# A graph layer's bias moved from TensorE to GpSimd, one slice product by seven, and a reordered last slice

## The chip, the cores and the metric

The kernel runs on one core of a Trainium2 chip. The metric is device time in microseconds (us), here the median of three runs. The engines are PE (TensorE, matrix products), DVE (VectorE), ACT (ScalarE), POOL (GpSimd) and SP (SyncE, which here only issues transfers). [...] All tensors are fp32, and every matmul appears in the records twice.

## The reference, cut to what matters

x is (8, 2048, 64): 8 batches, 2048 nodes, 64 features. Each of four layers computes `x = layernorm(x + layer(x, adj))`. The change concerns the first:

```python
# layer 0: A is adj (2048 x 2048), D = 16, K = 3
w = einsum('nd,dkio->nkio', embedding, weight)   # a weight of its own for each node
b = einsum('nd,do->no', embedding, bias)         # and a bias of its own
As = [eye, A, 2 * (A @ A) - eye]
x_g = einsum('knm,bmc->bnkc', stack(As), x)
out = einsum('bnki,nkio->bno', x_g, w) + b
x = layernorm(x + out)
```

Layers 1 to 3 multiply by adj five times more and project with small weights. The change does not touch them.

## The kernel before

Nodes lie on the 128 partitions in 16 tiles, and `xy[:, slot, tile, :]` holds two versions of x, with 8 batches of 64 features side by side as four pairs of 128 columns. A product with adj is computed by Strassen's method with seven products instead of eight (names A11, A12, A22, S1 to S4), and inside each of those once more by `inner`, so that 49 block products of 512 replace 64. The sums of blocks of adj that this needs are made once, while the first product runs, and kept in HBM (`comb`).

**The slices.** The first product, A x, reads adj in four slices `ns` of columns, each in four chunks `ch`. Slice 0 (`plain_slice`) is computed partly by plain products, partly by `two_level`, which computes a quarter by seven small products. Slices 1 to 3 go through `fast_slice`: A12, A22 (by `two_level`), A11 (plain, `mul`), S1, S2, S4 and S3, in this order on PE. The generator `prepare` makes the sums of adj on DVE, and stores them through POOL's queue; `fast_slice` takes it one step further with each `next(parts)`, so the order on DVE is written out by hand. The second half of slice 0's sums is made during slice 1 (`rest`). `done` adds a product in PSUM to a partial sum and writes the result `hT`; `keep_t1` stores it, `back` transposes it on PE into slot 1 of `xy` and `last_back` does that for the last two pairs after the slices end.

**The bias.** The layer's bias is made on PE: `biases` issues 16 matmuls of 16 partitions by 64 columns from `eT` and `bias0` into the two PSUM banks of `pb`, and `join_bias` adds it to a quarter of slot 0 on DVE, four times during and after the last slice (L766 to L770). Slot 0 is the accumulator of layer 0; `centered` then takes each quarter's mean off on DVE.

**The first big product and its features.** `product(1, ...)` (L1135) runs the seven `inner` products; each of these has seven groups of four matmuls of 512 columns (L277). Two banks `mm` take turns, so a bank must be read within about one group. During it, `feature0` handles 16 combinations of four tiles and one pair, in batches of 4, 4 and 8 between the `inner` products (`RUNS`, `pump.hold`). For each tile it computes the per-node weights' terms in two halves `y` (L1109, three buffers): half 0 is added to the accumulator by DVE (L1119), half 1 is scaled by ACT into one of two buffers `s` (L1123), and POOL adds `s` up and adds it to the accumulator (L1128, L1130). POOL also squares for the layernorm (L503).

**Order.** Loops are unrolled. A planner orders each engine's instructions by its own cost estimates and by program order; each engine then runs its list in order, waiting on semaphores. `tc.keep_in_program_order` puts an instruction behind the one written before it on its engine. `pump` is a queue of generators: each `pump.step` runs one step of the job in front, `pump.run(n)` runs n jobs to their end, and `hold` stops the steps.

Of the kernel before, what the change touches and what calls it, by code (L numbers as in the profile page):

```python
# [16 lines left out]
P = 128  # L17
EPS = 1e-5
GW = 512
# [85 lines left out]
def kernel(  # L105
# [6 lines left out]
    emb: bass.AP,  # L112
    embT: bass.AP,
    w_l0: bass.AP,
# [12 lines left out]
    D = emb.shape[2]  # L127
    F = b_l0.shape[1]
    B = BF // F
# [86 lines left out]
    def product(src, feature, between=None, rate=1, own=None, pin=False, runs=None, onto_slot=None, ends=False):  # L216
# [10 lines left out]
        def add(out, a, b, op=ALU.add):  # L227
            nc.vector.tensor_tensor(out, a, b, op)  # L228
            return out
# [7 lines left out]
        def inner(q, b, finish, early=None, tail=None, next_sum=None, home=None):  # L237
# [9 lines left out]
            def new():  # L247
                if places:
                    return places.pop(0)
                return sums.tile([P, TG, 2 * F], F32, tag="t", name="t", bufs=5)  # L250

            t1 = add(new(), b12, b11, ALU.subtract)
            t2 = add(new(), b22, t1, ALU.subtract)
            t3 = add(new(), b22, b12, ALU.subtract)
            t4 = add(new(), b21, t2, ALU.subtract)
            if next_sum is not None and home is None:
# [328 lines left out]
    if True:  # L585
# [48 lines left out]
        def prepare(ns, ch, outers):  # L634
# [26 lines left out]
            def raw(I, J):  # L661
                return [ch[2 * J + b][:, 2 * I + a] for a in range(2) for b in range(2)]
# [8 lines left out]
            def rq(I, J):  # L671
                return lambda c: ch[2 * J + c][:, 2 * I : 2 * I + 2]
# [11 lines left out]
            outers[A22] = inner(A22, *raw(1, 1))  # L684
            yield
            inner(A12, *raw(0, 1))
            if ns == 0:
# [3 lines left out]
                outers[A21] = inner(None, *raw(1, 0))  # L691
            outers[S1] = s1 = outer(rq(1, 0), rq(1, 1), ALU.add)
            outers[S2] = s2 = outer(sq(s1), rq(0, 0), ALU.subtract)
# [5 lines left out]
            put(S1, s1)  # L699
            yield  # L700
            put(S2, s2)
            if ns:
                inner(A11, *raw(0, 0))
            yield
            if ns:
                outers[S3] = s3 = outer(rq(0, 0), rq(1, 0), ALU.subtract)
                yield
            put(S3, s3)
            if ns == 0:
                yield  # L710
            put(S4, s4)
            yield

        with tc.tile_pool(name="p_n", bufs=4, space=PSUM) as p_n, tc.tile_pool(
            name="p_tn", bufs=2, space=PSUM
        ) as p_tn, tc.tile_pool(name="p_b", bufs=1, space=PSUM) as p_b, tc.tile_pool(
            name="xs", bufs=1
# [5 lines left out]
            for k in range(11):  # L723
                nc.tensor.matmul(rise[:, k % TG, :], zero, zero, start=True, stop=True)

            bias0 = small.tile([P, F], F32, tag="bias0", name="bias0")
            for k in range(2):
                nc.scalar.dma_start(bias0[k * F : k * F + D], b_l0)
            pb = p_b.tile([P, NT, F], F32, tag="pb", name="pb")
            e_tile = small.tile([P, TG, 4, F], F32, tag="sq", name="eT").rearrange("p t b f -> p (t b f)")  # L730
            eT = [e_tile[g // 2 * F : g // 2 * F + D, ts(g % 2, GW)] for g in range(NG)]
            for g in range(NG):
                nc.scalar.dma_start(eT[g], embT[:, ts(g, GW)])

            def biases():

                for t in (h * NT // 2 + k for k in range(NT // 2) for h in range(2)):
                    g = t // TG
                    tc.keep_in_program_order(nc.tensor.matmul(
                        pb[:, t, :], eT[g][:, ts(t % TG, P)], bias0[g // 2 * F : g // 2 * F + D],  # L740
                        start=True, stop=True,
                    ))
                yield

            def xq(h, c):
# [12 lines left out]
            def sums_of_x(n):  # L758
# [5 lines left out]
                pin(nc.vector.tensor_tensor(out, a, b, ALU.subtract))  # L764

            def join_bias(h, c):  # L766
                v = xq(h, c).rearrange("p t h (b f) -> p (t h) b f", f=F)
                bias = pb[:, h * NT // 2 : (h + 1) * NT // 2, :].unsqueeze(2)
                bias = bias.to_broadcast([P, NT // 2, B // 2, F])
                tc.keep_in_program_order(nc.vector.tensor_tensor(v, v, bias, ALU.add))  # L770

# [35 lines left out]
            ]  # L807
            t1 = [[by_tiles(xy[:, 1, c:NT:TG, ts(n, 2 * F)]) for n in range(4)] for c in range(2)]
            b4 = [T[3][:, 2 * j : 2 * j + 2, :, ts(p, 2 * F)] for j in range(2) for p in range(2)]
# [86 lines left out]
            def fast_slice(ns, ch, held, rest):  # L896
# [16 lines left out]

                def mul(ps, a, b, start=True, steps=2):

                    for p in range(2):
                        for k in range(NT // 2):
                            nc.tensor.matmul(  # L918
                                ps[:, ts(p, GW // 2)], b(k, p), a(k // TG, k % TG),
                                start=(start and p == k == 0), stop=(k == NT // 2 - 1),  # L920
                                skip_group_check=True,
                            )
                        if p < steps:
                            pump.step()
                    return ps
# [17 lines left out]

                next(parts)
                for _ in rest:
                    pass
# [10 lines left out]
                next(parts)  # L957
                pa = mul(bank(), raw(0, 0), x_of(0, 0))
                p1 = sums.tile([P, GW], F32, tag="p1", name="p1")
                nc.scalar.copy(p1, pa)  # L960
                nc.vector.tensor_tensor(q3, q3, p1, ALU.add)
                done(0, p2, p1)
                if ns == TG - 1:
                    join_bias(0, 1)
                next(parts)
# [3 lines left out]
                if ns == 1:  # L969
                    sum_weights(w3)  # L970
                elif ns == TG - 1:
                    join_bias(0, 0)
                pb_ = mul(bank(), summed(S2), t_of(2))
                u2 = plus("u2", pb_, p1)
                nc.vector.tensor_tensor(u2, pc, u2, ALU.add)
                nc.vector.tensor_tensor(p1, pc, p1, ALU.add)
                next(parts)
                pe = mul(bank(), summed(S4), x_of(1, 1))
                done(1, pe, u2)
                if ns == TG - 1:  # L980
                    join_bias(1, 0)
                mul(pb_, summed(S3), t_of(3), start=False)

                done(2, pb_, q3)
                done(3, pb_, p1)
                return [hT[p] for p in range(NP)]

            last_pairs = []
            for ns in range(TG):
                ch = [chunks.pop((ns, j)) for j in range(NG)]  # L990
                if ns == 0:
                    outers = {}
                    parts = prepare(ns, ch, outers)
                    for _ in range(2):
                        next(parts)
                    first4 = plain_slice(ns, ch, outers)
                    next(first4)
                    sums_of_x(0)
                    sums_of_x(1)
                    next(parts)  # L1000
                    next(first4)
                    sums_of_x(2)
                    sums_of_x(3)
                    sums_t(b4, t4)
                    next(first4)
                    next(parts)
                    hT = next(first4)
                    next(parts)
                    w3 = load_weights()
                    load_chunks(1, *AHEAD)  # L1010
                    pump.add(biases())
                else:
                    hT = fast_slice(ns, ch, held, parts if ns == 1 else ())
                for p in range(NP):
                    keep_t1(ns, p, hT[p])

                held = []
                for p in range(NP):
                    if ns == TG - 2:
                        held.append((ns, p, hT[p]))  # L1020
                    elif ns == TG - 1 and p >= NP // 2:
                        last_pairs.append(hT[p])
                    else:
                        pump.add(back(ns, p, hT[p]))
            join_bias(1, 1)
            pump.drain()
# [15 lines left out]
        if True:  # L1042
# [13 lines left out]
            pump.add(last_back())  # L1056
            for h, c in ((0, 0), (0, 1), (1, 1), (1, 0)):
                pump.add(centered(h, c))
            e_sb = l0y.tile([P, NT, D], F32, tag="e_sb", name="e_sb")
            nc.gpsimd.dma_start(e_sb, emb)  # L1060

            wn = l0y.tile([P, 3, D, F], F32, tag="wn", name="wn")
# [27 lines left out]
            def feature0(g, p, hT):  # L1090
# [7 lines left out]
                for k in range(TG):  # L1098
# [3 lines left out]

                    s = l0y.tile([P, DH, 2, F], F32, tag="s", name="s", bufs=2)
                    for h in range(2):
# [25 lines left out]
                    nc.gpsimd.tensor_tensor(acc, acc, s[:, 0], ALU.add)  # L1130
                    yield


# [132 lines left out]
```

## Time and profile before

| | us |
|---|---|
| median of 3 runs (1666.35 to 1666.91) | 1666.78 |
| the profiled execution | 1666.76 |
| its span, first to last instruction | 1665.0 |
| PE busy | 1656.7 |
| DVE busy | 965.9 |
| ACT busy | 276.0 |
| POOL busy | 246.1 |

The four slices and the products that follow stand in the profiled execution like this; the columns are busy time in us of three engines, and the mean share of the DMA engines.

| stretch (us) | what | PE | DVE | POOL | DMA |
|---|---|---|---|---|---|
| 0 to 59 | slice 0 | 57.94 | 40.79 | 9.81 | 0.88 |
| 59 to 111.1 | slice 1 | 51.79 | 48.06 | 12.70 | 1.00 |
| 111.1 to 160.5 | slice 2 | 49.40 | 33.05 | 10.41 | 0.93 |
| 160.5 to 211.7 | slice 3 | 50.86 | 41.06 | 10.99 | 0.85 |
| 211.7 to 309 | A11, S1, A12, S2 | 97.29 | 69.35 | 0.00 | 0.91 |
| 309 to 391.5 | four features | 82.50 | 45.74 | 45.00 | 0.13 |
| 391.5 to 439.8 | S4, S3 | 48.30 | 27.46 | 5.89 | 0.79 |
| 439.8 to 522.4 | four features | 82.60 | 45.77 | 45.08 | 0.12 |

Durations of single instructions overlap on PE, where one is recorded from its start to its modelled end; the time from one start to the next is what a matmul costs. In a line of the timeline, brackets give the idle time before the instruction and what ended it. In a group, the number after the bar is busy time, then the mean of one in ns, then the idle time before them.

### The profile page before, as it was taken

The page shows a single profiled execution, that of the slowest core. Times are in us where ns is not written, and L with a number is a line of the kernel's source. Part 1 is how long each engine was busy: PE and PEld are TensorE (multiplying, and loading weights), DVE is VectorE, ACT ScalarE, POOL GpSimd, SP SyncE. Part 2 cuts the span into 40 slices and gives each one's busy share as a digit, 9 for nine tenths or more (in the row PEclk, how much of TensorE's full clock was granted, in tenths as well). Part 3 has the DMA queues.
Part 4 walks back from the last instruction along what each step waited for, and adds up shares of the span by engine and source line. Part 5 has one row for each costly group of instructions (what it writes and reads, how often), then busy time and mean ns, then how long its engine had stood idle before and what let it go on. Part 6 is the DMA issues. An engine that isn't in the chain of part 4 may idle for free.

```text
span 1665.0 us, 21271 instructions
## 1 busy us (share of the span) xinstructions
PE 1656.7 (100%) x8414; PEld 1060.6 (64%) x8414; DVE 965.9 (58%) x1737; ACT 276.0 (17%) x810; POOL 246.1 (15%) x332
## 2 busy tenths in 40 slices
PE   9999999999999999999999999999999999999998
PEld 5988844444444444444454455599998455579998
DVE  5986895656456456655434365873668344453657
ACT  0200110242142144430010011220001011100001
POOL 1221200254155056550000000000000000000000
PEclk9999999999999999999999999999999999999999
DMA  8998899504503600019877867657888866678884
GB/s 318 340 383 310 316 322 326 200 26 162 205 26 129 250 26 26 26 65 364 290 266 278 304 254 257 229 218 272 291 297 299 306 209 233 230 264 294 316 311 167
DMA packets 81074, 391.56 MB, mean 235 GB/s; under 512 B 8944, under 2 KB 25584, under 8 KB 41040
## 3 DMA queue, kind: packets, MB, share of 16 engines
q1 hardware_dynamic: 68288, 346.78, 58.2%
q0 software_dynamic: 11248, 42.08, 6.7%
q10 hardware_dynamic: 1440, 1.35, 0.3%
q8 instruction: 67, 1.10, 0.3%
q14 instruction: 31, 0.25, 0.0%
HBM read 339.85 MB, written 50.33 MB: 234 GB/s over the span
## 4 chain that ended last, share of the span: by engine, by line
PE 95%; DVE 3%; DMA 1%; issue 0%; SPq 0%; DVEq 0%
PE y L1109 20%; PE mmb L277 17%; PE mma L277 12%; PE mmc L277 12%; PE mmb L270 9%; PE ps_n L918 7%; PE mma L270 6%; PE mmc L270 6%; PE z L1161 3%; PE z L1190 2%; PE ps_i L832 1%; DVE si L640 1%; DMA xy<-in_x 1%; PE pt L1152 1%; DMA bias<-in_b_l 0%; DVE so L640 0%
## 5 line engine op out<-in xcount | busy, mean ns | idle before, releaser
L277 PE MATMUL mmb<-a,t 128*128 128x512 f32 x648 | 292.0, 593 | 0.0
L1119 DVE SCALAR_TENSOR_TENSOR xy<-y,e_sb,xy 128x128 f32<-128x128 f32 x512 | 179.6, 351 | 141.2 <-PE y L1109 125.3
L277 PEld LDWEIGHTS mmb<-a,t 128*128 128x128 f32 x648 | 121.5, 190 | 145.3 <-issue 143.5
L1128 POOL TENSOR_TENSOR s<-s 128x512 f32<-128x512 f32 (+2 forms) x192 | 157.4, 820 | 333.0 <-ACT s L1123 322.8
L1123 ACT ACTIVATE s<-y,e_sb 128x128 f32<-128x128 f32 x512 | 139.3, 383 | 231.5 <-PE y L1109 231.5
L228 DVE TENSOR_TENSOR u<-mmb,p 128x512 f32<-128x512 f32 x84 | 57.9, 689 | 176.5 <-PE mmb L277 121.1
L270 PE MATMUL mmb<-t,a 128*128 128x128 f32 x1344 | 156.9, 275 | 0.0
L270 PEld LDWEIGHTS mmb<-t,a 128*128 128x128 f32 x1344 | 153.5, 192 | 0.0
L1109 PE MATMUL y<-wn,xT 64*128 64x512 f32 x512 | 131.5, 590 | 0.0
L1109 PE MATMUL y<-wn,C 64*128 64x512 f32 x512 | 131.2, 589 | 0.0
L1109 PE MATMUL y<-wn,tT 64*128 64x512 f32 x512 | 131.2, 589 | 0.0
L277 PE MATMUL mma<-a,T 128*128 128x512 f32 x256 | 115.5, 594 | 0.0
L277 PE MATMUL mmc<-a,t 128*128 128x512 f32 x216 | 97.3, 592 | 0.0
L295 ACT COPY p<-mma 128x512 f32<-128x512 f32 x42 | 24.7, 588 | 405.8 <-PE mma L277 248.4
L1109 PEld LDWEIGHTS y<-wn,xT 64*128 64x128 f32 x512 | 49.3, 187 | 61.2 <-issue 60.7
L1109 PEld LDWEIGHTS y<-wn,tT 64*128 64x128 f32 x512 | 49.6, 187 | 60.2 <-issue 60.2
L1109 PEld LDWEIGHTS y<-wn,C 64*128 64x128 f32 x512 | 49.5, 187 | 60.3 <-issue 60.3
L277 PE MATMUL mma<-a,xy 128*128 128x512 f32 x192 | 86.6, 594 | 0.3 <-PE pt_n L465 0.3
L277 PEld LDWEIGHTS mma<-a,T 128*128 128x128 f32 x256 | 47.6, 190 | 56.8 <-issue 56.5
L228 DVE TENSOR_TENSOR C<-mmc,C 128x512 f32<-128x512 f32 x48 | 33.2, 692 | 85.9 <-PE mmc L277 75.1
L277 PEld LDWEIGHTS mmc<-a,t 128*128 128x128 f32 x216 | 40.0, 190 | 45.4 <-issue 45.2
L277 PEld LDWEIGHTS mma<-a,xy 128*128 128x128 f32 x192 | 36.0, 190 | 44.4 <-issue 43.8
(160 smaller groups left out, 2127.5 us busy)
## 6 DMA issues: line engine op xcount, KB each, us to landing
a<-comb SPq DMA_DIRECT2D x240, 1024.0 KB, 4.8
a<-in_blocks SPq DMA_DIRECT2D x54, 1024.0 KB, 4.8
comb<-si POOLq DMA_DIRECT2D x28, 1024.0 KB, 6.2
a<-in_slices SPq DMA_DIRECT2D x15, 1024.0 KB, 9.0
comb<-so POOLq DMA_DIRECT2D x15, 512.0 KB, 9.6
t1T<-hT SPq DMA_DIRECT2D x16, 256.0 KB, 4.6
xT<-in_xT SPq DMA_DIRECT2D x16, 256.0 KB, 3.0
tT<-t1T SPq DMA_DIRECT2D x16, 256.0 KB, 3.1
```

The lines of the kernel that those rows point to most:

```text
L228: nc.vector.tensor_tensor(out, a, b, op)
L270: nc.tensor.matmul(to, a[:, k, m, :], xb[:, m, :], start=(start and opens and m == 0), stop=(m == TG - 1), skip_group_check=True,)
L277: nc.tensor.matmul(ps, xb[:, m, :], a[:, :, m, :], start=(start and m == 0), stop=(m == TG - 1), skip_group_check=True,)
L295: nc.scalar.copy(p1, pa)
L640: tc.keep_in_program_order(nc.vector.tensor_tensor(out, a, b, op))
L918: nc.tensor.matmul(ps[:, ts(p, GW // 2)], b(k, p), a(k // TG, k % TG), start=(start and p == k == 0), stop=(k == NT // 2 - 1), skip_group_ ...
L1109: mm = nc.tensor.matmul(y[:, b, :], terms[n][half, ts(k, P)], wn[half, n, h * DH : (h + 1) * DH, :], start=(n == 0), stop=(n == 2),)
L1119: nc.vector.scalar_tensor_tensor(acc, y[:, :, ts(d, F)], e, acc, ALU.mult, ALU.add)
L1123: nc.scalar.activation(s[:, d], y[:, :, ts(d, F)], AF.Copy, scale=e)
L1128: nc.gpsimd.tensor_tensor(s[:, :n], s[:, :n], s[:, n : 2 * n], ALU.add)
L1161: nc.tensor.matmul(z[:, k, :], aT[:, ts(k, P)], wd[:, w, :], start=(n == 0), stop=(n == len(terms) - 1),)
L1190: nc.tensor.matmul(z[n][:, k], xT[half, ts(k, P)], w[half], start=True, stop=True)
```

## The change

It has four parts.

1. The bias leaves PE, `pb` and `join_bias`. `biased(h)` makes it on POOL for eight tiles: it loads the bias row to all partitions (512 KB), takes its mean off on DVE (`center`, pinned), and for each tile multiplies by the embedding, adds up the 16 terms in four steps and adds the result to the accumulator. Its two tiles are the two buffers `s` of `feature0`. `biased(0)` is a job between `centered` of the first half and of the second; `biased(1)` runs at the end of the fourth feature. The six loads of `eT` and `bias0` are gone.
2. Slice 1's A11 goes through `two_level`. Its sums and S1 are made before the rest of slice 0's sums, of which S2 and S4 are now left (S4 alone before). `t1` swaps its two places in slot 1.
3. In slice 3, S3 runs ahead of S4, in a bank of its own; pairs 0 and 1 are complete after it and are transposed during S4, which uses a `p_tn` bank. `p_tn` has four banks instead of two, in place of `pb`.
4. The four differences at the start of an `inner` with a `home` are pinned.

```diff
@@ -249,10 +248,18 @@
...
-            t1 = add(new(), b12, b11, ALU.subtract)
-            t2 = add(new(), b22, t1, ALU.subtract)
-            t3 = add(new(), b22, b12, ALU.subtract)
-            t4 = add(new(), b21, t2, ALU.subtract)
+            pin = tc.keep_in_program_order if places else lambda inst: inst
+            def less(a, b):
+                out = new()
+                pin(nc.vector.tensor_tensor(out, a, b, ALU.subtract))
+                return out
+            t1 = less(b12, b11)
+            t2 = less(b22, t1)
+            t3 = less(b22, b12)
+            t4 = less(b21, t2)
             if next_sum is not None and home is None:
@@ -683,13 +690,19 @@
...
             yield
+            if ns == 1:
+                outers[A11] = inner(A11, *raw(0, 0))
+                outers[S1] = s1 = outer(rq(1, 0), rq(1, 1), ALU.add)
+                yield
             inner(A12, *raw(0, 1))
...
                 outers[A21] = inner(None, *raw(1, 0))
-            outers[S1] = s1 = outer(rq(1, 0), rq(1, 1), ALU.add)
+            if ns != 1:
+                outers[S1] = s1 = outer(rq(1, 0), rq(1, 1), ALU.add)
             outers[S2] = s2 = outer(sq(s1), rq(0, 0), ALU.subtract)
@@ -698,22 +711,23 @@
...
             yield
+            if ns == 0:
+                put(S3, s3)
+                yield
             put(S2, s2)
-            if ns:
+            if ns > 1:
                 inner(A11, *raw(0, 0))
...
                 yield
-            put(S3, s3)
-            if ns == 0:
-                yield
+                put(S3, s3)
             put(S4, s4)
...
         with tc.tile_pool(name="p_n", bufs=4, space=PSUM) as p_n, tc.tile_pool(
-            name="p_tn", bufs=2, space=PSUM
-        ) as p_tn, tc.tile_pool(name="p_b", bufs=1, space=PSUM) as p_b, tc.tile_pool(
+            name="p_tn", bufs=4, space=PSUM
+        ) as p_tn, tc.tile_pool(
             name="xs", bufs=1
@@ -722,26 +736,6 @@
...
                 nc.tensor.matmul(rise[:, k % TG, :], zero, zero, start=True, stop=True)
-            bias0 = small.tile([P, F], F32, tag="bias0", name="bias0")
-            for k in range(2):
-                nc.scalar.dma_start(bias0[k * F : k * F + D], b_l0)
-            pb = p_b.tile([P, NT, F], F32, tag="pb", name="pb")
-            e_tile = small.tile([P, TG, 4, F], F32, tag="sq", name="eT").rearrange("p t b f -> p (t b f)")
-            eT = [e_tile[g // 2 * F : g // 2 * F + D, ts(g % 2, GW)] for g in range(NG)]
-            for g in range(NG):
-                nc.scalar.dma_start(eT[g], embT[:, ts(g, GW)])
-            def biases():
-                for t in (h * NT // 2 + k for k in range(NT // 2) for h in range(2)):
-                    g = t // TG
-                    tc.keep_in_program_order(nc.tensor.matmul(
-                        pb[:, t, :], eT[g][:, ts(t % TG, P)], bias0[g // 2 * F : g // 2 * F + D],
-                        start=True, stop=True,
-                    ))
-                yield
             def xq(h, c):
@@ -763,12 +757,6 @@
...
-            def join_bias(h, c):
-                v = xq(h, c).rearrange("p t h (b f) -> p (t h) b f", f=F)
-                bias = pb[:, h * NT // 2 : (h + 1) * NT // 2, :].unsqueeze(2)
-                bias = bias.to_broadcast([P, NT // 2, B // 2, F])
-                tc.keep_in_program_order(nc.vector.tensor_tensor(v, v, bias, ALU.add))
             def load_chunks(ns, *js):
@@ -805,7 +793,7 @@
...
             ]
-            t1 = [[by_tiles(xy[:, 1, c:NT:TG, ts(n, 2 * F)]) for n in range(4)] for c in range(2)]
+            t1 = [[by_tiles(xy[:, 1, 1 - c : NT : TG, ts(n, 2 * F)]) for n in range(4)] for c in range(2)]
             b4 = [T[3][:, 2 * j : 2 * j + 2, :, ts(p, 2 * F)] for j in range(2) for p in range(2)]
@@ -911,7 +899,7 @@
...
-                def mul(ps, a, b, start=True, steps=2):
+                def mul(ps, a, b, start=True, steps=2, n=1):
@@ -921,7 +909,7 @@
...
                         if p < steps:
-                            pump.step()
+                            pump.step(n)
                     return ps
@@ -942,6 +930,8 @@
...
                 next(parts)
+                if ns == 1:
+                    next(parts)
                 for _ in rest:
@@ -955,34 +945,47 @@
...
                 next(parts)
-                pa = mul(bank(), raw(0, 0), x_of(0, 0))
-                p1 = sums.tile([P, GW], F32, tag="p1", name="p1")
-                nc.scalar.copy(p1, pa)
+                p1 = new_out("p1")
+                if ns == 1:
+                    two_level(
+                        lambda i, j: lambda m: ch[j][:, m, i], outers[A11], b1[0], t1[0], by_blocks(p1)
+                    )
+                else:
+                    pa = mul(bank(), raw(0, 0), x_of(0, 0))
+                    nc.scalar.copy(p1, pa)
                 nc.vector.tensor_tensor(q3, q3, p1, ALU.add)
                 done(0, p2, p1)
-                if ns == TG - 1:
-                    join_bias(0, 1)
                 next(parts)
...
                     sum_weights(w3)
-                elif ns == TG - 1:
-                    join_bias(0, 0)
                 pb_ = mul(bank(), summed(S2), t_of(2))
...
                 nc.vector.tensor_tensor(u2, pc, u2, ALU.add)
-                nc.vector.tensor_tensor(p1, pc, p1, ALU.add)
-                next(parts)
-                pe = mul(bank(), summed(S4), x_of(1, 1))
-                done(1, pe, u2)
                 if ns == TG - 1:
-                    join_bias(1, 0)
-                mul(pb_, summed(S3), t_of(3), start=False)
-                done(2, pb_, q3)
-                done(3, pb_, p1)
+                    nc.vector.tensor_tensor(q3, pb_, q3, ALU.add)
+                    next(parts)
+                    ps3 = mul(bank(), summed(S3), t_of(3))
+                    done(2, ps3, q3)
+                    for p in range(2):
+                        keep_t1(ns, p, hT[p])
+                        pump.add(back(ns, p, hT[p]))
+                    done(3, ps3, u2)
+                    pe = p_tn.tile([P, TG, P], F32, tag="pt", name="ps_e").rearrange("p t n -> p (t n)")
+                    mul(pe, summed(S4), x_of(1, 1), n=2)
+                    done(1, pe, u2)
+                else:
+                    nc.vector.tensor_tensor(p1, pc, p1, ALU.add)
+                    next(parts)
+                    pe = mul(bank(), summed(S4), x_of(1, 1))
+                    done(1, pe, u2)
+                    mul(pb_, summed(S3), t_of(3), start=False)
+                    done(2, pb_, q3)
+                    done(3, pb_, p1)
                 return [hT[p] for p in range(NP)]
@@ -1005,24 +1008,21 @@
...
                     hT = next(first4)
-                    next(parts)
                     w3 = load_weights()
                     load_chunks(1, *AHEAD)
-                    pump.add(biases())
                 else:
                     hT = fast_slice(ns, ch, held, parts if ns == 1 else ())
-                for p in range(NP):
+                for p in range(0 if ns < TG - 1 else 2, NP):
                     keep_t1(ns, p, hT[p])
...
                         held.append((ns, p, hT[p]))
-                    elif ns == TG - 1 and p >= NP // 2:
+                    elif ns < TG - 1:
+                        pump.add(back(ns, p, hT[p]))
+                    elif p >= 2:
                         last_pairs.append(hT[p])
-                    else:
-                        pump.add(back(ns, p, hT[p]))
-            join_bias(1, 1)
             pump.drain()
@@ -1054,10 +1054,33 @@
...
             pump.add(last_back())
-            for h, c in ((0, 0), (0, 1), (1, 1), (1, 0)):
-                pump.add(centered(h, c))
             e_sb = l0y.tile([P, NT, D], F32, tag="e_sb", name="e_sb")
             nc.gpsimd.dma_start(e_sb, emb)
+            def new_s():
+                return l0y.tile([P, DH, 2, F], F32, tag="s", name="s", bufs=2)
+            def biased(h):
+                b, terms = (new_s().rearrange("p a b f -> p (a b) f") for _ in range(2))
+                nc.gpsimd.dma_start(b.rearrange("p d f -> p (d f)"), b_l0.to_broadcast([P, D * F]))
+                center(b, pin=tc.keep_in_program_order)
+                for t in range(h * NT // 2, (h + 1) * NT // 2):
+                    e = e_sb[:, t].unsqueeze(2).to_broadcast([P, D, F])
+                    nc.gpsimd.tensor_tensor(terms, b, e, ALU.mult)
+                    n = D // 2
+                    while n:
+                        nc.gpsimd.tensor_tensor(terms[:, :n], terms[:, :n], terms[:, n : 2 * n], ALU.add)
+                        n //= 2
+                    acc = xy[:, 0, t].rearrange("p (b f) -> p b f", f=F)
+                    nc.gpsimd.tensor_tensor(acc, acc, terms[:, :1].to_broadcast([P, B, F]), ALU.add)
+                yield
+            for h, c in ((0, 0), (0, 1)):
+                pump.add(centered(h, c))
+            pump.add(biased(0))
+            for h, c in ((1, 1), (1, 0)):
+                pump.add(centered(h, c))
@@ -1129,6 +1152,10 @@
...
                     yield
+                if (g, p) == order[TG - 1]:
+                    for _ in biased(1):
+                        pass
```

## The prediction

> **What bounds the kernel now.** I read the busy shares first, then who PE waited for over the whole span.
>
> ```profile
> PE 1656.7 (100%) x8414; PEld 1060.6 (64%) x8414; DVE 965.9 (58%) x1737; ACT 276.0 (17%) x810; POOL 246.1 (15%) x332
> ```
>
> ```profile
> PE rise L724 <- DVE zero L721: 1.1, 1, 1.1
> PE ps_i L832 <- DVE si L640: 0.3, 1, 0.3
> PE mma L277 <- PE pt_n L465: 0.3, 1, 0.3
> ```
>
> PE is the bound and waits 1.7 us in all. Only two things can pay: matmuls taken out, and those two 0.3 us waits. Against that, each microsecond in which PE waits for something new is paid in full. POOL, 15% busy, is where work is added, so I read the timeline of PE, DVE, ACT and POOL where the change touches it.
>
> ```profile
> 62.51 2.00 PE L739 MATMUL pb<-bias,eT 16*128 16x64 f32 x32
> 69.37 1.13 PE L832 MATMUL ps_i<-si,t 128*128 128x128 f32 x8 [0.31 <-DVE si L640]
> 90.37 7.07 PE L918 MATMUL ps_n<-so,T 128*128 128x256 f32 x32
> 100.25 0.68 DVE L941 TENSOR_TENSOR u<-ps_n,p 128x512 f32<-128x512 f32 x1
> ...
> 209.99 1.45 PE L465 MATMUL pt_n<-ident,hT 128*128 128x128 f32 x8
> 211.71 3.67 PE L277 MATMUL mma<-a,xy 128*128 128x512 f32 x8 [0.27 <-PE pt_n L465]
> ```
>
> Columns are start, duration, engine and operation. The reader sees the bias matmuls, PE's wait in slice 1, a 32-record product, the DVE read of the S2 product, and the hand-over from the slices to the first product.
>
> **What PE gains.** The 16 bias matmuls go: next product starts at 64.44, so 1.93 us. A11 of slice 1 by seven products: a plain product takes 6.91 us from start to start (90.37 to 97.28), a seven-product one 6.25 (167.45 to 173.70): 0.66. The wait at 69.37: unhindered groups follow every 0.89, so this one was due at 68.89 and 0.48 was lost. In the new order slice 0's S2 sums (2.5 us of DVE) stand behind slice 1's A22 sums, which end their second step near 66.7; PE wants it at 67.2. I take 0.48. At the hand-over PE passes from S3's end (209.99) to 211.71, 1.72 us, of which the eight transposes need 0.86; now they stand within the S4 product, whose first half (3.46 us) covers the two DVE adds of 0.42 before them and whose second half covers the two ACT copies of 0.53. Gain 0.86.
>
> **What DVE takes back in slice 1.** DVE has no idle time from 23.76 to 107.9. Up to the read of the S2 product it does all it did and two more adds (0.55 and 0.42, rows L847 and L850): the read moves from 100.25 to 101.2 and ends at 101.95. PE, earlier by 3.1 us with one transpose group before A22, comes to S3 at 100.86, and S3 adds into the bank that is being read. It waits 1.09 (nothing at best; 2 if the planner puts more ahead). Sum so far: -1.93 - 0.66 - 0.48 - 0.86 + 1.09 = -2.84 us.
>
> **Edits I cost at nothing.** The four bias adds on DVE (9.1 us): PE never waited for them, and the first work of the product waits for a transpose (L417). The six early loads dropped on ACT's queue, 136 KB, are at best 0.4 us at the 326 GB/s of slice 0. Slice 0's S2 and S4 stores leave POOL's queue up to 11 us later, slice 2's chunks are freed 2.6 and 1.2 us later; they were issued from 81.23 and first used at 111, and a store takes 6.2 us to land, read over 100 us later. If that cover failed, PE would wait for the difference, 1 to 3 us. The four pinned differences now run during S4, ahead of need.
>
> **What POOL takes on.** These groups price it, and the timeline shows what it meets.
>
> ```profile
> L1128 POOL TENSOR_TENSOR s<-s 128x512 f32<-128x512 f32 x64 | 81.1, 1268 | 322.9 <-ACT s L1123 322.8
> L1128 POOL TENSOR_TENSOR s<-s 128x256 f32<-128x256 f32 x64 | 47.1, 736 | 5.0
> L1128 POOL TENSOR_TENSOR s<-s 128x128 f32<-128x128 f32 x64 | 29.2, 456 | 5.0
> L503 POOL TENSOR_TENSOR sq<-xy 128x1024 f32<-128x1024 f32 x8 | 15.8, 1976 | 0.6
> ```
>
> ```profile
> 396.54 1.38 DVE L228 TENSOR_TENSOR C<-C,p 128x512 f32<-128x512 f32 x1 [0.69 <-ACT p L295]
> 399.65 2.22 POOL L503 TENSOR_TENSOR sq<-xy 128x1024 f32<-128x1024 f32 x1
> 400.04 2.37 DVE L228 TENSOR_TENSOR C<-C,u 128x512 f32<-128x512 f32 x1
> 439.75 1.13 PE L1109 MATMUL y<-wn,xT 64*128 64x512 f32 x4
> 445.28 2.18 ACT L1123 ACTIVATE s<-y,e_sb 128x128 f32<-128x128 f32 x8 [25.39 <-PE y L1109]
> ```
>
> One tile of `biased` is a multiply of 1024 columns, adds of 512, 256, 128 and 64, and an add of 512. The multiply has no row: 1.98 by the square (one tensor read twice), 2.35 by the slope of the s adds (2.1 ns a column); I take 2.15. The add of 64 is 0.32 by that slope. With 0.075 between operations (three adds of 2.45 fill 2.60): 2.15 + 1.27 + 0.74 + 0.46 + 0.32 + 1.27 + 0.45 = 6.65 us a tile, 53 us for eight, twice.
>
> The second call, `biased(1)`, follows the fourth feature and takes both `s` buffers. PE turns from features to S4 at 391.5 and back at 439.75, and ACT wants an `s` at 445.28. The buffer of tile 2 is free at 391.95. Loading `b` (512 KB) lands in 3.6 us by the smallest bias row, 10.3 by a 512 KB store on the same queue; I take 6. Its centring (1.21 and 1.22) ends at about 400.5, and the square has POOL until 401.9. The last read of `b` comes after seven tiles and a multiply, 48.7 us: 450.6. Now the collision: a DVE add of two SBUF tensors, 0.69 undisturbed, took 1.38 and 2.37 because it began under a POOL operation, and the POOL operation after it came 0.33 late (the square 2.22 for 1.89). Sixteen such adds lie between 402 and 451: 5.3 us, so 455.9. ACT needs 2.2 more to empty one `y`: 458.2. PE, with three `y` buffers, one held by ACT, can do five halves of 2.58 from 439.75, until 452.6 (four, 450.1, if the next in turn is the blocked one). It waits 5.6 us. Bounds: nothing (load in 3.6, no collisions: `y` free at 448), and 18 (load in 10.3, multiply 2.35, a whole add of 0.68 lost each of 16 times, four halves).
>
> [...]
>
> The first call, `biased(0)`, runs from about 239 to 300, after centring is done and before ACT's first `s` at 314: no buffer is waited for. But it lies under a DVE that is full at 228 to 250 and at 285 to 298.
>
> ```profile
> 244.77 0.69 DVE L228 TENSOR_TENSOR u<-mmb,p 128x512 f32<-128x512 f32 x1
> 292.81 0.68 DVE L228 TENSOR_TENSOR u<-mmb,p 128x512 f32<-128x512 f32 x1
> ```
>
> Both reads already start 1.0 us after their product's end; PE needs the bank one group (3.43) after that end, so they may be 2.6 late. Ahead of the first come the new centring (2.43) and two collisions of 0.7, ahead of the second five: 4.9 and 4.5 late, PE waits 2.3 and 1.9. That holds if nothing is planned differently; the planner may put these reads first, and then it is nothing. I take the middle, 2.0 (0 to 5).
>
> **Sum.** -2.84 + 5.6 + 2.0 = +4.8 us on the profiled execution's 1666.76 us (span 1665.0 and 1.76 around it; the median of the runs is 1666.78): 1671.5.
>
> **Rivals.**
> 1. POOL stays covered: `b` lands quickly and the planner keeps DVE's small reads first. Then only -2.84 is left, 1663.9; with slice 1's S3 wait gone too, 1662.8. For it: POOL's 53 us meet 48.3 us of products plus 13 us of features, nearly enough. Against it: the collisions are in the trace.
> 2. The bill is larger: `b` is queued behind S4's block loads (DMA 0.79 busy there), and the pinned centring makes DVE wait for it. Behind it on DVE stand S4's reads of `mm` banks; PE stands still from 2.6 us of lateness on. With the 18 us bound or 10 us of mixed waits: 1674 to 1682.
> 3. Slice 1's DVE queue decides instead: chunk loads or a store slip, PE loses 3 us there and POOL is covered: 1666 to 1668.
>
> **How the numbers follow.** A measurement of this kernel can tell about 0.2%, 3.3 us, from no change. The forecast (waits for POOL of 4 to 10 us) has 0.45, rival 1 0.27, rival 2 0.18, rival 3 0.10. Faster by over 0.2% means under 1663.4, the better half of rival 1: 0.12. Within 0.2%, to 1670.1: the rest of rival 1, rival 3 and the forecast's lower edge, 0.31. Slower: 0.57. The range of eight in ten runs from 1663.2 to 1681; the forecast's own from 1668 to 1674.
>
> **What would show it.** Right: in the changed trace PE waits for ACT `s` (or `y`) near 450, POOL is busy without a break for 50 to 60 us after the fourth feature, DVE two-tensor adds take 1 to 2.4 us inside both POOL stretches, PE's last slice product runs straight into `mma`, and DVE's S2 read in slice 1 holds S3 back by about 1 us. Wrong: no PE wait in the feature batches, or POOL's multiply well under 2 us.

## The result, and the profile after

| | before | after |
|---|---|---|
| median of the runs, us | 1666.62 (1666.35 to 1666.91) | 1676.84 (1675.97 to 1678.63) |
| ratio, 95% interval | | 1.0063 [1.0045, 1.008] |
| the profiled execution, us | 1666.76 | 1678.63 |
| its span, us | 1665.0 | 1676.8 |

The change makes the kernel 10.2 us slower: inside the range on record, on the forecast's side, and twice as far as the forecast's 4.8. The forecast's own band, 1668 to 1674, is missed; the time lies in the one given to rival 2. Two executions at a lower granted clock (1723.93 us of the kernel before, at 0.948, and 1922.12 of e5b_fill6, at 0.85) are in no ratio below. The same kernel in a second profiled execution (a2_after below) has a span of 1676.0. The stretches of PE, from the starts of the first matmul of each, in us:

| stretch | before | after | second execution | forecast of the difference |
|---|---|---|---|---|
| slice 0 | 58.96 | 60.08 | 59.30 | 0 |
| slice 1 | 52.13 | 48.80 | 48.80 | -1.98 |
| slices 2, 3 | 100.62 | 99.86 | 99.87 | -0.86 |
| A11, S1, A12, S2 | 97.18 | 100.65 | 100.66 | +2.0 |
| four features | 82.60 | 82.61 | 82.60 | 0 |
| S4, S3 | 48.26 | 50.64 | 49.23 | 0 |
| four features | 82.61 | 91.51 | 92.89 | +5.6 |
| the rest | 1142.64 | 1142.65 | 1142.65 | 0 |

Slice 0 is no cost: the first execution waited 1.4 us for x to arrive, and in the experiments below slice 0 ends at 58.64 to 59.39. The first line of the page, and who PE waited for (in total, times, longest):

```profile
PE 1656.7 (99%) x8406; PEld 1057.8 (63%) x8406; DVE 987.4 (59%) x1739; ACT 276.8 (17%) x816; POOL 369.1 (22%) x430
```

```profile
PE y L1132 <- ACT s L1146: 5.8, 1, 5.8
PE mmc L284 <- DVE C L227: 2.9, 2, 2.1
PE mmb L284 <- DVE u L227: 1.9, 2, 1.2
```

PE's busy time is the same to a tenth although PE has 2.6 us less to do (the bias and a plain product made by seven): matmuls at half clock count as busy for longer (twelve records 5.28 us for 2.58, below). The two waits of before (for `si`, for `pt_n`) are gone; three kinds took their place. The timeline of the slices:

```profile
96.79 0.69 DVE L929 TENSOR_TENSOR u<-ps_n,p 128x512 f32<-128x512 f32 x1
205.28 3.62 PE L906 MATMUL ps_e<-so,xy 128*128 128x256 f32 x16
208.74 3.60 PE L284 MATMUL mma<-a,xy 128*128 128x512 f32 x8
```

The read of S2's product stands among small work at 96.79, not at 101, so S3 waits for nothing; and the last slice product runs into `mma` without a gap. Then the second call of `biased`, on PE, DVE, POOL and ACT, put together from one timeline for each engine:

```profile
392.73 0.59 POOL L1066 DMA_DIRECT2D s<-in_b_l  x1 [0.30 <-POOL xy L1153]
402.98 2.35 POOL L1070 TENSOR_TENSOR s<-s,e_sb 128x1024 f32<-128x1024 f32 x1
403.50 2.38 DVE L227 TENSOR_TENSOR C<-C,u 128x512 f32<-128x512 f32 x1
408.11 3.70 PE L284 MATMUL mmc<-a,t 128*128 128x512 f32 x8 [2.11 <-DVE C L227]
452.18 1.02 PE L1132 MATMUL y<-wn,C 64*128 64x512 f32 x4
454.87 1.90 POOL L1070 TENSOR_TENSOR s<-s,e_sb 128x1024 f32<-128x1024 f32 x1
456.80 2.17 ACT L1146 ACTIVATE s<-y,e_sb 128x128 f32<-128x128 f32 x8 [34.03 <-POOL s L1070]
459.02 2.08 PE L1132 MATMUL y<-wn,xT 64*128 64x512 f32 x4 [5.82 <-ACT s L1146]
460.89 1.92 PE L1132 MATMUL y<-wn,tT 64*128 64x512 f32 x4
```

The last multiply (454.87) is the last reader of `b`, which lies in a buffer `s`; ACT's first `s` waits for it, and PE for ACT. What comes after the wait was in no forecast: four records take 1.87 and 1.71 us instead of 0.86. The windows (us, then PE, PEld, DVE, ACT and POOL busy, PE's granted clock, DMA share, GB/s) say why:

```profile
440.00:453.00 13.00, 13.00 (x55) 5.48 (x53) 10.41 (x19) 0.00 (x0) 12.21 (x11) 1.00 0.46 167
453.10:459.00 5.90, 0.11 (x2) 0.00 (x0) 0.60 (x2) 2.17 (x8) 5.48 (x6) 0.91 0.00 0
459.00:464.30 5.30, 5.28 (x12) 2.20 (x14) 0.00 (x0) 2.17 (x8) 4.91 (x8) 0.50 0.00 0
```

The clock fell to 0.50 within the wait and stayed there for the next twelve records: 5.28 us for what takes 2.58.

### The profile page after: what moved, and what is told of

Its sections match the earlier page's. It is cut to its first block, busy times and chain, and to the rows that moved or that the text cites. A ratio compares the mean times of both kernels' runs of the same rounds, so it can differ in the third digit from the quotient of the medians.

```text
span 1676.8 us, 21379 instructions
## 1 busy us (share of the span) xinstructions
PE 1656.7 (99%) x8406; PEld 1057.8 (63%) x8406; DVE 987.4 (59%) x1739; ACT 276.8 (17%) x816; POOL 369.1 (22%) x430
## 4 chain that ended last, share of the span: by engine, by line
PE 81%; DVE 2%; POOL 1%; DMA 0%; issue 0%; ACT 0%; DVEq 0%; POOLq 0%
PE y L1132 19%; PE mmb L284 15%; PE mmc L284 11%; PE mma L284 10%; PE mmb L277 9%; PE mma L277 6%; PE mmc L277 6%; PE z L1188 3%; PE z L1217 2%; PE pt L1179 1%; POOL s L1073 0%; POOL s L1070 0%; DVE C L227 0%; DMA s<-in_b_l 0%; DVE wm L596 0%
## 5 line engine op out<-in xcount | busy, mean ns | idle before, releaser
L1188 PEld LDWEIGHTS z<-wd,C 128*128 128x128 f32 x384 | 50.2, 191 | 21.8 <-issue 20.8
```

The costliest lines, as they stand in the source:

```text
L1188: nc.tensor.matmul(z[:, k, :], aT[:, ts(k, P)], wd[:, w, :], start=(n == 0), stop=(n == len(terms) - 1),)
```

## The experiments

Each is the changed kernel with one edit, unless it says otherwise. Ratios are to the kernel before, with 95% intervals. The theory: POOL's arithmetic costs all of it, by holding `s` (with a half clock behind the wait) and by delaying DVE. The rivals: the load of `b` and its centring; or slice 1 and the last slice.

**1. Without the bias (e1_no_bias).** Both calls of `biased` go.

```diff
-            pump.add(biased(0))
...
-                if (g, p) == order[TG - 1]:
-                    for _ in biased(1):
-                        pass
```

> The changed kernel without both calls of biased, so layer 0's bias is left out; parts 2 to 4 of the change stay. Theory (all of the loss comes from the bias on POOL, by the held s buffers and by collisions with DVE): features take 82.6 us per batch of four, A11 to S2 97.2, S4 and S3 48.3, PE reaches the first product near 208.7, and the kernel takes about 1663.8 us in all, 14.8 less than the profiled execution of the changed kernel minus its own overhead. Rival (the reordered slices or the four p_tn banks cost something later): 1667 or more, with PE waits left in the products.

Measured: 1663.50 us, ratio 0.9977 [0.9967, 0.9988]. The first product starts at 208.05 and the four stretches behind it take 97.11, 82.60, 48.26 and 82.60. All that PE waits for:

```profile
PE rise L738 <- DVE zero L735: 1.1, 1, 1.1
PE ps_n L860 <- DMA xy<-in_x: 0.8, 1, 0.8
```

So parts 2 to 4 and the removal from PE gain 3.2 us, and the whole loss lies in `biased`: 1676.84 - 1663.50 = 13.3 us. How that divides is read by windows of 230 to 302 (first call) and 402.9 to 461.2 (second call), first of the changed kernel, then of e1_no_bias:

```profile
230.00:302.00 72.00, 69.25 (x160) 29.96 (x159) 60.18 (x51) 2.34 (x4) 67.39 (x48) 1.00 0.93 320
402.90:461.20 58.30, 50.37 (x142) 21.90 (x142) 39.05 (x51) 2.97 (x10) 54.61 (x50) 0.97 0.62 220
```

```profile
230.00:302.00 72.00, 72.00 (x169) 31.88 (x168) 46.68 (x54) 2.34 (x4) 0.00 (x0) 1.00 0.93 326
402.90:461.20 58.30, 58.30 (x196) 25.95 (x196) 28.59 (x62) 9.29 (x33) 10.56 (x14) 1.00 0.57 207
```

In the first window DVE is busy 13.5 us longer with three records fewer. PE, full without POOL, is 2.75 us short there.

**2. Load and centring alone (e2_load_center).** POOL's arithmetic goes, the bias is left out; a copy of 64 columns keeps the load and the centring alive.

```diff
-                for t in range(h * NT // 2, (h + 1) * NT // 2):
...
+                nc.gpsimd.tensor_copy(terms[:, :1], b[:, :1])
```

> The changed kernel with only the load of the bias row and its centring on DVE left of biased, and one copy of 64 columns on POOL; the multiplies and adds of the bias are left out. Theory (POOL's operations collide with DVE's two-tensor adds): A11 to S2 takes 97.2 to 98 us, S4 and S3 48.3 to 49, the second batch of features 82.6, 1664 to 1665 in all. Rival (it is the centring's 2.4 us on DVE and DVE's wait for the load that make PE wait): 100.6 and 50.6 stay as in the changed kernel, 1670 in all.

Measured, in one execution: 1663.8 us, span 1662.0. A11 to S2 takes 97.10, S4 with S3 49.05, the second four features 82.60. One wait is new:

```profile
PE mmc L284 <- DVE C L227: 0.5, 1, 0.5
```

The rival is small: by themselves, the load and the centring cost 0.8 us at S4 and nothing elsewhere. The other 3.5 us of A11 to S2 and everything in the features is POOL's arithmetic.

**3. The second call in two (e3_split).** Four tiles after the fourth feature and four after the eighth; `b` is loaded and centred once more.

```diff
-            def biased(h):
+            def biased(first, count):
...
-                for t in range(h * NT // 2, (h + 1) * NT // 2):
+                for t in range(first, first + count):
...
-                if (g, p) == order[TG - 1]:
-                    for _ in biased(1):
-                        pass
+                for n in range(2):
+                    if (g, p) == order[(n + 1) * TG - 1]:
+                        for _ in biased(NT // 2 + n * TG, TG):
+                            pass
```

> biased for the second half of the tiles is split: four tiles after the fourth feature, four after the eighth. Nothing is left out. Theory (the loss in the second batch is the hold of the two s buffers beyond the 48 us of products): each stretch of POOL work ends about 28 us after it starts, so ACT finds s free, the second batch takes 82.6 instead of 91.5, and the time is 1668 us if the collisions stay as they are, up to 1671 if the second stretch costs A22 another 2.4. Rival (POOL's total work counts, wherever it lies): 1675 to 1677.

Measured: 1669.66 us, ratio 1.0017 [1.0007, 1.0026]. The second four features take 82.60, as before; A11 to S2 still 100.66, S4 with S3 50.54, and the stretch after the features loses 0.7. Its waits:

```profile
PE mmc L284 <- DVE C L227: 3.3, 3, 2.0
PE mmb L284 <- DVE u L227: 1.9, 2, 1.2
PE rise L738 <- DVE zero L735: 1.1, 1, 1.1
```

The wait for `s` is gone, and with it the half clock (the mean granted clock of the span is 1.000, against 0.997 in the changed kernel). This shows the hold of `s`: the same eight tiles, on the same engine, cost 8.9 us less in that stretch when only four at a time have to fit into the 48 us of S4 and S3.

**4. POOL busy without reading (e6_memset).** In each tile POOL's seven operations become seven fills of 1024 columns; the bias is left out.

```diff
-                for t in range(h * NT // 2, (h + 1) * NT // 2):
...
+                nc.gpsimd.tensor_copy(terms[:, :1], b[:, :1])
+                for t in range(NT // 2):
+                    for _ in range(7):
+                        nc.gpsimd.memset(terms, 0.0)
```

> The changed kernel with POOL's multiplies and adds of the bias replaced by seven fills of 1024 columns for each tile (a fill of 896 columns took 0.85 us), so that POOL is busy for about as long but reads no SBUF; the bias is left out. Theory (DVE's two-tensor adds collide with POOL's reads): DVE's adds keep 0.69 us inside both stretches, A11 to S2 takes 97.2 us and S4 with S3 about 49; the wait for the second s buffer is 0 to 3 us. Rival (any POOL instruction blocks them): the adds take 1 to 2.4 us and the products 100.6 and 50.6 as in the changed kernel.

Measured, in one execution: 1671.38 us, span 1669.4. POOL, and DVE's add of two SBUF tensors that took 2.38 us in the changed kernel:

```profile
399.21 56.47 POOL L1071 MEMSET s<- 128x1024 f32 x56
```

```profile
404.91 0.69 DVE L227 TENSOR_TENSOR C<-C,u 128x512 f32<-128x512 f32 x1
```

A11 to S2 takes 97.10 again and S4 with S3 49.18. So it is not POOL's being busy that holds DVE back: DVE's add takes 0.69 beside the fills, which only write SBUF, and 2.38 beside the multiply, which also reads it. The run does not part the reading from the arithmetic, which the fills leave out as well. The second part was a miss: a fill takes 1.01 us, so that the stand-in was as long as the real arithmetic, and PE waited 5.6 us for `s` (expected 0 to 3), with the half clock in and behind it; the window covers the wait:

```profile
452.30:457.90 5.60, 0.04 (x2) 0.00 (x0) 0.53 (x2) 2.18 (x8) 5.27 (x7) 0.70 0.00 0
```

It is a second case of the hold, without the collisions. Here the fills hold only one of the two buffers, and PE did six halves before the wait instead of four.

**5. PE kept busy through the wait (e5_fill, e5b_fill6, e5c_fill6).** Matmuls of 128x512 whose result nobody reads are put after the last features that PE can do before the wait; twelve in the first kernel, six in the others, which are the same kernel twice.

```diff
+    FILL = 6
...
+                        if (g, p) == order[TG] and k == h == 1:
+                            fill = p_mm.tile([P, GW], F32, tag="mm", name="fill")
+                            for _ in range(FILL):
+                                tc.keep_in_program_order(nc.tensor.matmul(
+                                    fill, ident, xy[:, 1, 0, :GW], start=True, stop=True
+                                ))
```

> The changed kernel with 12 matmuls of 512 columns more (24 records, 5.15 us at full clock) on PE in the place where it waits for s, after the second tile of the fifth feature; their result is not used. Theory (after 5.8 us without work the granted clock was 0.5 for 6.8 us, and this doubled 12 records): PE is busy until 458, waits less than 1 us, the clock stays at 1.00, the second batch takes 88.9 instead of 91.5 us, and the time is 1674 us. Rival (those records are slow because the y buffers come back slowly): the 12 records still take 5.3 us, no gain, 1676 to 1677.

Measured with twelve: 1680.01 us, ratio 1.0076 [1.006, 1.0092].

```profile
451.77 10.57 PE L1143 MATMUL fill<-xy,ident 128*128 128x512 f32 x24
462.26 1.13 PE L1133 MATMUL y<-wn,xT 64*128 64x512 f32 x4
463.23 1.02 PE L1133 MATMUL y<-wn,tT 64*128 64x512 f32 x4
```

A miss in time: a record costs 0.43 us, twice what was expected (the price was taken from the features' matmuls of 64 rows; the products of 128 rows show 3.43 us for eight records). The filling was longer than the wait. But the records behind it ran at full pace, so six were tried.

> The filler again with 6 matmuls instead of 12: a record of a filler matmul on 128 rows took 0.43 us, not the 0.215 of the features' records on 64 rows, so 12 records are 5.15 us. Theory (idle time halves the clock): PE is busy until about 457, waits about 1 us or less for ACT, the 12 records after it take 2.6 us instead of 5.3, the granted clock stays at 1.00, the second batch takes 88.9 us instead of 91.5, and the time is 1674.2 us. Rival (a wait of 1 us is enough to halve the clock): the 12 records take 5.3 us and the time is that of the changed kernel, 1676.8.

> The changed kernel with six matmuls of 128x512 that nothing reads, on PE between the last features it can do and the wait for s: 12 records of 0.43 us, 5.2 us of work in a wait of 5.8. Theory (the half clock after the wait is due to PE standing idle): PE waits at most 1 us for s, the clock stays at 1.00, the 12 records after it take 2.6 us instead of 5.3, the batch of four features takes 88.5 to 89 us instead of 91.5, and the median is 1674 to 1675. Rival (the half clock is due to something else at that point, such as the transfers or POOL's work): the clock falls to 0.5 with PE busy, the batch takes 91.5 and the median is 1676 to 1677.

Measured with six: ratios 1.0053 [1.0038, 1.0068] and 1.0051 [1.0037, 1.0065], the second with a median of 1674.85 us. Timeline and window of e5c_fill6:

```profile
452.35 5.42 PE L1143 MATMUL fill<-xy,ident 128*128 128x512 f32 x12
458.25 1.13 PE L1133 MATMUL y<-wn,xT 64*128 64x512 f32 x4 [0.49 <-ACT s L1153]
459.22 1.02 PE L1133 MATMUL y<-wn,tT 64*128 64x512 f32 x4
```

```profile
452.00:459.00 7.00, 6.51 (x18) 2.69 (x18) 0.87 (x3) 2.18 (x8) 6.45 (x8) 1.00 0.00 0
```

`s` comes when it came, POOL and ACT do what they did, the clock stays at 1.00, and the twelve records take 2.68 us. The batch takes 88.70 against 91.51 and 92.89. Useless work makes the kernel 2.1 us faster (1674.85 against 1676.91 in the same comparison). At this point the clock fell to 0.50 with PE idle for 5.8 and 7.2 us, and stayed at 1.00 with PE idle for 0.5: the half clock is here the price of PE standing idle.

**6. The changed kernel again (a2_after).**

> The changed kernel once more, unaltered, for its slice 0, its wait for s and its clock. Theory: the first transfer is not waited for as long as in the first profile (1.6 us), so slice 0 ends at 58.8 to 59.4 instead of 60.08; the wait for s in the second batch of four features is again 5.5 to 6.1 us, a granted clock of 0.5 for 6.8 us follows a few us after it began, and the 12 records after the wait again take 5.2 to 5.3 us; median 1676.0 to 1677.5. Rival (the half clock was a chance of that one execution): the wait is the same, the 12 records take 2.6 us, and the median is 1674 or its spread is over 2.5 us.

Measured: 1676.91 us, ratio 1.0062 [1.0046, 1.0077]. Slice 0 ends at 59.30, the twelve records take 5.28 again. The wait was expected at 5.5 to 6.1 and was 7.17:

```profile
458.20 2.08 PE L1132 MATMUL y<-wn,xT 64*128 64x512 f32 x4 [7.17 <-ACT s L1146]
```

```profile
451.00:458.20 7.20, 0.03 (x2) 0.00 (x0) 0.52 (x2) 2.18 (x8) 6.65 (x8) 0.69 0.00 0
458.20:463.50 5.30, 5.30 (x14) 2.22 (x16) 0.00 (x0) 2.18 (x8) 4.91 (x8) 0.50 0.00 0
```

S4 with S3 was 1.41 us shorter in this execution and the wait 1.35 longer: what DVE's collisions cost PE there is time that PE would else have waited for `s`. The two don't add. From the end of the fourth feature to the restart of PE it is 67.02 us in one execution (392.00 to 459.02) and 66.97 in the other (391.23 to 458.20): POOL sets that time.

**7. The version that keeps the bias on PE (v1_pe_bias, v2_banks).** The kernel before with parts 2 and 3 only. In v1_pe_bias S4 of the last slice uses one of the banks `p_n` (PSUM, where the products lie), since `pb` takes the place of the two extra banks of `p_tn`; in v2_banks `p_tn` is opened ahead of `p_n`, so that `mma` gets another bank.

```diff
-        with tc.tile_pool(name="p_n", bufs=4, space=PSUM) as p_n, tc.tile_pool(
-            name="p_tn", bufs=2, space=PSUM
-        ) as p_tn, ...
+        with tc.tile_pool(name="p_tn", bufs=2, space=PSUM) as p_tn, tc.tile_pool(
+            name="p_n", bufs=4, space=PSUM
+        ) as p_n, ...
```

> The kernel before with parts 2 and 3 of the change alone: the bias stays on PE and in pb, slice 1's A11 goes by seven products, slice 3 runs S3 ahead of S4. S4 uses a p_n bank, p_tn keeps two, the four differences are not pinned. Nothing is left out. Theory (the gain of the reordered slices is independent of where the bias is made): slice 1 gains 1.4 us (3.3 in the changed kernel less 1.93 for the bias matmuls), the hand-over 0.8, the products and features take 97.2, 82.6 and 48.3 as before: 1664.6 us. Rival (DVE has no room in slices 1 and 3 for the bias adds beside the new order): PE waits for DVE there or at the hand-over and the time is 1666 to 1668.

Measured: 1665.62 us, ratio 0.9994 [0.9985, 1.0003]: no difference from before. The hand-over, on PE and DVE:

```profile
209.86 0.76 DVE L949 TENSOR_TENSOR hT<-ps_n,u 128x256 f32<-128x256 f32 x2 [0.17 <-PE ps_n L933]
210.71 1.52 PE L285 MATMUL mma<-a,xy 128*128 128x512 f32 x3 [0.90 <-PE ps_n L933]
```

The transposes no longer stand between S4 and `mma`, but `mma` is the bank that S4 was computed in, and DVE reads it until 210.62: the wait has only changed its name.

> v1_pe_bias with one difference: the PSUM pool p_tn is opened ahead of p_n, so that the first product's bank mma is not one that slice 3's S4 was computed in and DVE reads last. In v1_pe_bias PE ended S4 at 209.8 and began mma at 210.71 after waiting 0.90, while DVE read S4's bank from 209.86 for 0.76. Theory (that bank alone held mma back): the 0.90 goes, the first product starts at 209.8, and the median is 0.9 under v1_pe_bias, 1664.6 to 1664.8, ratio 0.9988 to 0.9990. Rival (mma waits for something else too, a transpose's copy or the banks of pb): the wait stays at 0.5 to 0.9 with another name, and the median is 1665.2 to 1665.7.

Measured: 1664.58 us (1664.20 to 1665.30, 11 runs), ratio 0.9988 [0.998, 0.9997].

```profile
205.89 3.62 PE L933 MATMUL ps_n<-so,xy 128*128 128x256 f32 x16
209.35 3.60 PE L285 MATMUL mma<-a,xy 128*128 128x512 f32 x8
```

That bank alone held `mma` back. In this execution slice 1 takes 50.93 us (1.20 less than before), slices 2 and 3 together 99.78 (0.84 less), and the products 97.10 and 48.26. This version is ahead of both kernels; against the kernel before by 0.12%, which the interval tells from nothing, barely. What the bias costs on PE is the distance to e1_no_bias: 1.1 us by the medians, 1.8 by the two ratios (1.93 were reckoned).

## Why the prediction was right in sign and short in size

**What PE gains.** Slice 1 gave 3.33 us where 1.93 + 0.66 + 0.48 = 3.07 were reckoned; the hand-over 0.76 for 0.86. e1_no_bias and v2_banks show these terms without POOL. The 1.09 us for S3's wait in slice 1 didn't come: the planner put the read of S2's product ahead of part of the small work (96.79), the lower bound of that step. The two edits costed at nothing which could show (stores later in POOL's queue, chunks freed later) show no wait.

**The second call.** The chain was right: load, centring, a square, eight tiles, ACT, PE. The load took 4.8 us (6 taken); from POOL's first multiply to the last read of `b` it is 53.79 us, where 48.7 + 5.3 = 54.0 stood. That sum was right by two errors: an undisturbed tile takes 6.40 (6.65 taken; its multiply 1.90 for 2.15), so seven take 44.8, and the collisions in the 51.89 us from the first multiply to the last are 7.1, not 5.3. POOL's own loss is thus 0.44 for each of the 16 adds that the prediction counted, nearer to the 0.33 of the rows than to the whole add of 0.68 in its upper bound. In one case the multiply of 2.23 us at 411.26 (1.90 undisturbed) came while a DVE add was running (410.57 to 411.73): 0.47 was left of it, and the multiply lost 0.33.

**The step that failed: what a wait costs PE.** The prediction took PE out of `y` after five halves, and charged the wait at its length, 5.6 us. Three things are off in it. PE did four halves (442.64 to 453.04), which the prediction had as its other case: 2.58 more. The collisions in S4 and S3, for which it had no term, come out of the wait and cost nothing of their own. And 2.9 us of half clock stand behind the wait (2.70 in the twelve records, 0.2 in the four behind them), for which the prediction had no term; in the kernel before no wait of PE was over 1.1 us. Together 8.9 + 2.4 = 11.3 us from the fourth feature on in one execution, 10.3 + 1.0 = 11.3 in the other, for 5.6. Part of this was hidden by luck: slice 1 and the hand-over gave 4.1 us, where 2.84 stood in the sum.

Of the half clock the runs show this. It lasted 6.83 us in the changed kernel, 10.24 in a2_after and 6.8 in e6_memset, from within waits of 5.8, 7.2 and 5.6 us, and with PE busy (e5c_fill6) there was none. It began 4.7 us into the first wait, 2.7 into the second and 2.2 into the third. A wait of 2.1 us, in S4, left the clock at 1.00. The kernel before has it too, where it costs nothing: PE's last matmul ends at 1658.43 us, and from 4.0 us later to the end of the span the clock is 0.50. A sum that has PE idle for 5.6 us could have carried a term for this, though no row of before gives its size.

**The first call.** 3.5 us (2.0 taken, bounds 0 to 5), in three waits of PE:

```profile
251.72 3.70 PE L284 MATMUL mmb<-a,t 128*128 128x512 f32 x8 [0.74 <-DVE u L227]
294.36 3.70 PE L284 MATMUL mmb<-a,t 128*128 128x512 f32 x8 [1.18 <-DVE u L227]
298.90 3.70 PE L284 MATMUL mmc<-a,t 128*128 128x512 f32 x8 [0.83 <-DVE C L227]
```

The three starts come 0.9, 1.3 and 1.1 us late. Of the two reads that the prediction named, only the second held PE up (294.36). The first came in time, at 242.66; the next read of that bank, at 250.99, was the late one, so the place was off by one read. e6_memset shows that it is collisions. The call lasts 71 us against 53 reckoned, 20 us over eight undisturbed tiles, but nobody waits for its end.

**The rivals.** Rival 1 (POOL covered) fell with the first wait; e1_no_bias, 1663.50, is the time that it gave (1663.9). Rival 3 has nothing for it: slice 1 waits for nothing. Rival 2's bill (1674 to 1682) holds the time, but its mechanism, the load and DVE's waits for it, costs 0.8 us by e2_load_center. Its other place, the late reads of `mm` banks in S4, is there (2.11 us), and lies within the time that POOL sets.

## What to carry to other kernels

Work that is moved to an idle engine is paid where it holds something: here a buffer that PE's chain needs soon after 48 us of products, against 54 us of work until its last read; splitting the same work in two took that away (1676.84 us to 1669.66). Count a long wait of PE (5.6 us and more here, not 2.1) as the wait and the half clock behind it (1.8 to 3.0 us here), and first find which engine sets the time of the restart: delays on the way there don't add to it. Where two phases meet, look at which PSUM bank the next one starts in; one bank's last read was 1.0 us here, half of the 1.9 us that v2_banks is ahead of the kernel before.

## What the runs showed of the hardware that was not expected

- With waits of 5.8, 7.2 and 5.6 us PE's granted clock was 0.50 for 6.83, 10.24 and 6.8 us, begun within the waits, which cost 1.8 to 3.0 us beyond the wait itself; six unread matmuls in the wait kept it at 1.00.
- POOL's fills of SBUF left DVE's adds of two SBUF tensors at 0.69 us; POOL's adds and multiplies, which also read it, took them up to 2.38. POOL suffers too, and by more than the rows of before showed: four adds of a tile, 2.99 us undisturbed, took 7.51 where DVE was full:

```profile
243.73 7.51 POOL L1073 TENSOR_TENSOR s<-s 128x512 f32<-128x512 f32 x4
456.85 2.99 POOL L1073 TENSOR_TENSOR s<-s 128x512 f32<-128x512 f32 x4
```
